# First kernels on VectorE with the lengths' tables behind them, later chunks' exponentials on GpSimd, and products of ones ahead of the first strip

## The chip, the cores and the metric

One core of a Trainium2 chip runs the whole program. The metric is the device time in microseconds (us), as the median of several runs. TensorE (PE) multiplies matrices, VectorE (DVE), ScalarE (ACT) and GpSimd (POOL) work on tiles of up to 128 partitions, and SyncE's queue (SP) issues most transfers.

## The reference

For 128 sequences (B) of 32 heads (H) and 512 positions (L) the reference does three things.

- It makes one convolution kernel of 512 taps for each head from a diagonal state space model: `K[h, l] = 2 Re sum_n Ct[h, n] exp(dtA[h, n] * l)` over 64 complex states n, with `dtA = (-exp(log_A_real) + i A_imag) * dt` and `Ct = C (exp(dtA) - 1) / A`.
- It convolves each row `x[b, h, :]` causally with `K[h]`, adds `D[h] * x`, and sets positions at and beyond the sequence's length to zero.
- It passes the 4096 rows of 512 values through a mixture of experts: sigmoid gates with a bias, the best 4 of 16 experts with normalised weights, a gated network `silu(x Wg) * (x Wu) Wd` of inner width 256 for each, plus one shared expert. The result is added to x.

```python
dtA = A * dt[:, None]
Ct = Cc * (jnp.exp(dtA) - 1.0) / A
P = dtA[:, :, None] * jnp.arange(length)
K = 2.0 * jnp.einsum('hn,hnl->hl', Ct, jnp.exp(P)).real
...
y = irfft(rfft(u, n=2*L) * rfft(K, n=2*L))[..., :L] + u * D[:, None]
y = y * mask[:, None, :]
...
out = x + experts(y)
```

## The kernel before

**Kernels of the heads.** States lie on partitions: 128 partitions hold the 64 states of two heads, so 32 heads are 16 column pairs. `CHUNKS = ((0, 2), (2, 4), (6, 4), (10, 6))` cuts these pairs into four chunks of 2, 4, 4 and 6, that is heads 0 to 3, 4 to 11, 12 to 19 and 20 to 31. A tap l is split into 16a + b, so that 32 + 16 = 48 values (`lab`) per pair are enough: a chunk's tiles are 128 x 96, 192, 192 and 288, and chunk 0 has 16 more columns in front (`lead`), from which `Ct` is made.

`waves` makes a chunk's exponentials. The angle part (L306, then `reduce_angle`, L244 to L248, then L316) works on `wr` and `wk` on VectorE, and ScalarE takes sine and cosine (L317, L322). The size part starts with a product on GpSimd (L309, into `wv`), goes through `exp_parts` on VectorE (L254 to L263: clamp, two steps for the exponent, two for the remainder, one for the scale `ws`, seven for the series `wq`) and ends in L325 (`wm`). All these tiles have one buffer. `kernels` then multiplies size by cosine and sine into `f_r`, `f_i` (L373, L374) and `ge_r`, `ge_i` (L381, L382), multiplies by `Ct` (L385 to L390, half of it on GpSimd), and TensorE sums over the states into `pk` (L394). VectorE adds the skip term into `krow` (L402), and SP writes it to DRAM as `kd` (L409). `kernel_strip` (L419) reads `kd` back as 128 shifted copies, the Toeplitz strip of four heads: in four transfers for heads 0 to 3, in one of 1 MB after that, with two buffers.

**The lengths' tables.** L429 to L512 rank the sequences by length, and make `to_rank`, `to_row`, `within` and, from them, `by_rank`, `reach`, `k_u` and `unit_rows`. The convolution needs only `within` and `to_rank`; `to_row` goes into `route`, and the others are used after the last head.

**The convolution.** It runs over 8 blocks (`tb`) of 4 heads. For each head TensorE multiplies four pieces of the transposed x with the strip (`py`, L520), VectorE masks by length (`yb`, L527), TensorE transposes with `to_rank` (`pt`, L530), and ScalarE copies to `store` (L531). After a block come the gates on TensorE (`parts` L549, `pg` L560), and after every second block `route` on VectorE, which finds the best four experts. Chunks 1, 2 and 3 are made after heads 0, 2 and 5 in the order of the program. Strip `tb + 1` is loaded at the first head of block `tb`.

**Order.** Up to the last head the order of each engine's instructions is not written out: a scheduler places each one at build time from the order of the program and its own estimate of when operands are ready. Each engine then runs its list strictly in that order. After the convolution come the shared expert in eight units, the table of slots, and the experts' tiles, with orders written out by hand. The change does not touch them, but for where four of their tables are made.

Of the kernel before, what the change touches and what calls it, by code (L numbers as in the profile page):

```python
# [38 lines left out]
P = 128  # L39
# [15 lines left out]
ONE_HOTS = 8  # L55
AHEAD = 4
# [19 lines left out]
def ssm_moe_kernel(  # L76
# [76 lines left out]


# [95 lines left out]
    def exp_parts(v, q, k, s):  # L250

        nc.vector.tensor_scalar(v, v, -87.0, 88.0, ALU.max, ALU.min)  # L254
        nc.vector.tensor_scalar(k, v, 1.0 / math.log(2.0), ROUND, ALU.mult, ALU.add)  # L255
        nc.vector.tensor_scalar(k, k, ROUND, None, ALU.subtract)
        for part in (LN2_1, LN2_2):
            nc.vector.scalar_tensor_tensor(v, k, -part, v, ALU.mult, ALU.add)
        nc.vector.tensor_scalar(q, v, SERIES[0], None, ALU.mult)
        for c in SERIES[1:]:  # L260
            nc.vector.scalar_tensor_tensor(q, q, c, v, ALU.add, ALU.mult)  # L261

        nc.vector.tensor_scalar(s, k, 127.0, 2.0**23, ALU.add, ALU.mult)  # L263
# [13 lines left out]
    def wide(name, w, dtype=F32, most=WMAX):  # L277
        return ks1.tile([P, most], dtype, tag=name, name=f"{name}{w}")[:, :w]
# [16 lines left out]
    def waves(c0, n, lead):  # L295
# [3 lines left out]
        v, r, k, q = (wide(t, w) for t in ("wv", "wr", "wk", "wq"))  # L299
        s, mag = wide("ws", w, I32), wide("wm", w)  # L300

        def pairs(t):
            return t[:, lead:].rearrange("p (c x) -> p c x", x=NX)

        by_l = lab.unsqueeze(1).to_broadcast([P, n, NX])
        nc.vector.tensor_mul(  # L306
            pairs(r), by_l, dta_i[:, c0 : c0 + n].unsqueeze(2).to_broadcast([P, n, NX])
        )
        nc.gpsimd.tensor_mul(  # L309
            pairs(v), by_l, dta_r[:, c0 : c0 + n].unsqueeze(2).to_broadcast([P, n, NX])  # L310
        )
        if lead:
            nc.vector.tensor_copy(r[:, :lead], dta_i)
            nc.vector.tensor_copy(v[:, :lead], dta_r)
# [8 lines left out]
        exp_parts(v, q, wide("we", w), s)  # L323
        s = s.bitcast(F32)
        nc.vector.scalar_tensor_tensor(mag, q, 1.0, s, ALU.add, ALU.mult)  # L325
        return tuple(pairs(t) for t in (mag, k, r)), (mag, q, s, r, half)

    first, (mag, q, s, r, half) = waves(*CHUNKS[0], NC2)
# [38 lines left out]
    def kernels(c0, n, mag, cos, sin):  # L367

        cs = slice(c0, c0 + n)

        for j in range(2):
            rows = slice(j * N, (j + 1) * N)
            nc.vector.tensor_mul(f_r[rows, cs, j, :], cos[rows, :, LA:], mag[rows, :, LA:])  # L373
            nc.gpsimd.tensor_mul(f_i[rows, cs, j, :], sin[rows, :, LA:], mag[rows, :, LA:])  # L374
# [6 lines left out]
        nc.vector.tensor_mul(e_r, cos[:, :, :LA], mag[:, :, :LA])  # L381
        nc.gpsimd.tensor_mul(e_i, sin[:, :, :LA], mag[:, :, :LA])  # L382
# [3 lines left out]
        nc.gpsimd.tensor_mul(g_t, e_i, by_i)  # L386
        nc.vector.tensor_add(g_r, g_r, g_t)
        nc.vector.tensor_mul(g_i, e_r, by_i)
        nc.gpsimd.tensor_mul(e_i, e_i, by_r)
# [12 lines left out]
        nc.vector.tensor_add(  # L402
# [7 lines left out]
        for h in range(2 * c0, 2 * (c0 + n)):  # L410
            kd_of[h] = kd[h - 2 * c0 : h - 2 * c0 + 1, :]

# [12 lines left out]
    kernels(*CHUNKS[0], *first)  # L425
    kernel_strip(0)


    len_col = const.tile([P, 1], F32, tag="len_col", name="len_col")  # L429
    nc.vector.tensor_copy(len_col, len_col_i)  # L430
    key_row = const.tile([P, B], F32, tag="key_row", name="key_row")
    nc.vector.tensor_copy(key_row, len_row_i)
    key_col = const.tile([P, 1], F32, tag="key_col", name="key_col")
    for key, raw, own in ((key_row, key_row, cpos), (key_col, len_col, ppos)):
        nc.vector.tensor_scalar(key, raw, 0.0, float(L), ALU.max, ALU.min)
        if key is key_col:
            num_len = const.tile([P, 2], F16, tag="num_len", name="num_len")
            nc.vector.tensor_copy(num_len[:, 0:1], ppos)
# [16 lines left out]
    to_rank_h = const.tile([P, P], F16, tag="to_rank_h", name="to_rank_h")  # L455
    nc.vector.tensor_copy(to_rank_h, to_rank)

    by_rank_ps = ps_m.tile([P, 2], F32, tag="m", name="by_rank_ps")
    nc.tensor.matmul(by_rank_ps, lhsT=to_rank_h, rhs=num_len, start=True, stop=True)
    by_rank = const.tile([P, 2], F32, tag="by_rank", name="by_rank")  # L460
    nc.vector.tensor_copy(by_rank, by_rank_ps)


    reach = const.tile([P, KT], BF16, tag="reach", name="reach")
    nc.vector.memset(reach, 1.0)
    for n in range(1, KT):
        nc.vector.tensor_scalar(
            reach[:, n : n + 1], by_rank[:, 1:2], float(n * P), None, ALU.is_gt
        )

    unit = const.tile([P, NU], BF16, tag="unit", name="unit")
    nc.vector.tensor_scalar(unit, upos, 0.0, None, ALU.is_equal)
    reach_sum = const.tile([P, 1], F32, tag="reach_sum", name="reach_sum")
    nc.vector.tensor_reduce(reach_sum, reach, AX.X, ALU.add)
    reach_b = const.tile([P, 1], BF16, tag="reach_b", name="reach_b")
    nc.vector.tensor_copy(reach_b, reach_sum)
    k_u_ps = ps_m.tile([1, NU], F32, tag="m", name="k_u_ps")
    nc.tensor.matmul(k_u_ps, lhsT=reach_b, rhs=unit, start=True, stop=True)
    k_u = const.tile([1, NU], I32, tag="k_u", name="k_u")
    nc.vector.tensor_copy(k_u, k_u_ps)  # L480


    div = const.tile([P, 2], F32, tag="div", name="div")
# [367 lines left out]
    def dep(of, on, why):  # L851
        tc.add_manual_dep(of.ins, on.ins.name, SYNC, reason=why)
# [345 lines left out]
```

## Time and profile before

| | |
|---|---|
| median of 3 runs | 956.56 us (956.15 to 957.12) |
| the profiled execution | 961.51 us, its span 959.8 us |
| last `pt` of the convolution done | about 139.5 us |
| `krow` of chunk 0 done, first `py` | 22.39 us, 27.09 us |
| busy over the span | PE 93%, VectorE 45%, GpSimd 45%, ScalarE 18% |
| granted TensorE clock, mean | 0.985 |

A row of the timeline has the start in us, the duration in us, engine, line, operation, output and inputs, and in brackets the idle time before it with what ended it. The rows of windows give, for each stretch, its length and the busy time of PE, PE weight loads, VectorE, ScalarE and GpSimd with their numbers of instructions, then the granted clock, the share of the transfer engines that was busy, and GB/s. The shares over the whole span say little here, since the change lies in the first 100 us.

### The profile page before, as it was taken

Reading aid. Unit: us, or ns where it says so; the run is one execution under the profiler, and the core shown is the slowest. Engines: PE = TensorE matmul, PEld = TensorE weight load, DVE = VectorE, ACT = ScalarE, POOL = GpSimd, SP = SyncE. Lnnn points to the kernel's source line nnn. Section 1 sums busy time; section 2 is a strip of 40 time slices with the busy share of each in tenths; the row PEclk is TensorE's granted clock in tenths of the full one; section 3 lists DMA queues with packets and bytes.
Section 4 is the critical chain, followed back from the end, with each engine's and each line's share of the span. In section 5 each row is a group of like instructions: output and inputs, shape, how many; then the busy total and the mean of one; then the engine's idle time right before and its main releaser. Section 6 shows DMA issues by size and latency. Waiting matters only on the chain.

```text
span 959.8 us, 14544 instructions
## 1 busy us (share of the span) xinstructions
PE 890.6 (93%) x2960; PEld 443.3 (46%) x2960; DVE 427.6 (45%) x1438; ACT 171.3 (18%) x343; POOL 432.0 (45%) x400
## 2 busy tenths in 40 slices
PE   0799994989998999999999999999999999999995
PEld 0455652344444444444444444444444544444442
DVE  7955555868762233443334233423433323334332
ACT  1122221000001012221222122212222112222211
POOL 4210002033456545664556455655555445556644
PEclk9999997989999999999999999999999999999998
DMA  4467732164456676687667766766666646677755
GB/s 161 126 228 265 233 125 68 66 223 151 165 193 196 251 166 111 127 138 164 113 119 140 166 109 120 137 108 106 125 121 114 112 90 113 112 119 138 131 110 104
DMA packets 54032, 135.94 MB, mean 142 GB/s; under 512 B 12784, under 2 KB 12944, under 8 KB 51344
## 3 DMA queue, kind: packets, MB, share of 16 engines
q0 software_dynamic: 35616, 89.77, 47.5%
q1 hardware_dynamic: 14064, 36.15, 11.4%
q10 hardware_dynamic: 4224, 8.39, 2.3%
q8 instruction: 71, 1.16, 0.5%
q14 instruction: 57, 0.47, 0.1%
HBM read 288.08 MB, written 52.25 MB: 355 GB/s over the span
## 4 chain that ended last, share of the span: by engine, by line
PE 78%; DVE 15%; issue 3%; another core or an unknown queue 1%; DMA 1%; POOL 1%; ACT 0%; SPq 0%; DVEq 0%; POOLq 0%; ACTq 0%
PE g L1044 33%; PE o L1070 24%; PE m L1012 4%; PE o L930 3%; PE u L1062 3%; PE py L520 3%; PE u L904 2%; DVE cols L794 2%; PE g L904 2%; DVE rows L793 1%; DVE yb L527 1%; PE pt L530 1%; DVE wq L261 1%; PE parts L549 1%
## 5 line engine op out<-in xcount | busy, mean ns | idle before, releaser
L1044 PE MATMUL g<-store,yt 128*128 x742 | 343.1, 596 | 4.1 <-ACT yt L1018 2.7
L1080 POOL DMA_INDIRECT out<-xg,put x134 | 212.1, 1583 | 236.5 <-DVE junk L1019 203.2
L1070 PE MATMUL o<-store,zT 128*128 x536 | 252.2, 593 | 1.3 <-DVE zT L1065 1.3
L1056 DVE SCALAR_TENSOR_TENSOR zt<-g,wt,sgt 128x256 f32<-128x256 f32 x135 | 65.3, 483 | 287.0 <-ACT sgt L1055 272.6
L1044 PEld LDWEIGHTS g<-store,yt 128*128 128x128 f32 x742 | 130.3, 190 | 121.0 <-issue 116.8
L1070 PEld LDWEIGHTS o<-store,zT 128*128 128x128 f32 x536 | 101.3, 190 | 130.5 <-issue 124.3
L869 POOL DMA_INDIRECT yg<-y_rows,get x140 | 138.8, 991 | 42.8 <-issue 30.2
L1079 DVE COPY xg<-o 128x512 f32<-128x512 f32 x134 | 92.7, 692 | 110.3 <-PE o L1070 109.4
L1018 ACT COPY yt<-m 128x512 f32<-128x512 f32 x136 | 79.6, 586 | 238.1 <-PE m L1012 225.9
L1055 ACT ACTIVATE sgt<-g 128x256 f32<-128x256 f32 x135 | 51.9, 384 | 268.6 <-PE g L1044 227.8
L1012 PEld LDWEIGHTS m<-ident,yg 128*128 128x128 f32 x373 | 48.5, 141 | 73.2 <-issue 73.0
L520 PE MATMUL py<-strip,xt 128*128 128x512 f32 (+3 forms) x256 | 77.7, 443 | 5.0 <-DMA strip<-kd 5.0
L918 POOL DMA_INDIRECT xg<-in_x,unit_rows x32 | 31.1, 970 | 108.9 <-DVE sig_k L255 99.5
L939 POOL DMA_INDIRECT out<-xg,unit_rows x32 | 31.5, 984 | 98.6 <-DVE xg L937 90.4
L930 PE MATMUL o<-store,z 128*128 128x512 f32 x128 | 60.5, 622 | 6.1 <-DVE xg L937 6.1
L1012 PE MATMUL m<-ident,yg 128*128 128x128 f32 x373 | 63.3, 273 | 1.1 <-issue 1.1
L1065 DVE COPY zT<-u 128x256 f32<-128x256 f32 x134 | 56.3, 420 | 0.1
L520 PEld LDWEIGHTS py<-strip,xt 128*128 128x128 f32 x256 | 41.9, 194 | 21.8 <-issue 9.3
L1062 PE MATMUL u<-ident,zt 128*128 128x128 f32 x268 | 51.2, 273 | 0.0
L904 PE MATMUL g<-store 128*128 128x512 f32 x92 | 44.5, 621 | 0.7 <-ACT store L531 0.7
L904 PE MATMUL u<-store 128*128 128x512 f32 x92 | 42.9, 601 | 0.8 <-issue 0.8
L930 PEld LDWEIGHTS o<-store,z 128*128 128x128 f32 x128 | 24.8, 199 | 38.0 <-issue 28.0
(272 smaller groups left out, 519.7 us busy)
## 6 DMA issues: line engine op xcount, KB each, us to landing
store<-in_w_all SPq DMA_DIRECT2D x143, 1536.0 KB
xt<-in_x_t SPq DMA_DIRECT2D x8, 1024.0 KB
y_rows<-yb ACTq DMA_DIRECT2D x8, 1024.0 KB
strip<-kd SPq DMA_DIRECT2D x7, 1024.0 KB
yg<-y_rows,get POOLq DMA_INDIRECT x140
out<-xg,put POOLq DMA_INDIRECT x134
strip<-kd SPq DMA_DIRECT2D x4, 256.0 KB
xg<-in_x,unit_rows POOLq DMA_INDIRECT x32
```

The costliest lines, as they stand in the source:

```text
L520: nc.tensor.matmul(py[:, : L - jt * P], lhsT=xt[:, jt, q, :], rhs=strip[tb][:, q, jt * P :], start=(jt == 0), stop=(jt == KT - 1),)
L869: nc.gpsimd.indirect_dma_start(out=at(yg, t), out_offset=None, in_=y_rows[:, :], in_offset=bass.IndirectOffsetOnAxis(ap=made["get"][:, t : ...
L904: nc.tensor.matmul(ps[it], lhsT=w_sh[:, c0 : c0 + P], rhs=yT[:, u, kt, :, :].rearrange("p h b -> p (h b)"), start=(kt == KT - n), stop=(kt ...
L930: nc.tensor.matmul(po, lhsT=at(zu, u)[:, it, q * P : (q + 1) * P], rhs=w_sh[:, c0 : c0 + L], start=(it == 0), stop=(it == IT - 1),)
L1012: nc.tensor.transpose(pt[:, q, :], at(yg, t)[:, q * P : (q + 1) * P], ident)
L1018: nc.scalar.copy(at(yt, t), pt)
L1044: mm = nc.tensor.matmul(pgu, lhsT=at(yt, t)[:, q, :], rhs=ring_flat[:, bass.ds(w0s[t] + q * 2 * I, 2 * I)], start=(q == KT - n), stop=(q = ...
L1056: nc.vector.scalar_tensor_tensor(at(zs, t), pgu[:, I:], at(wts, t), sg, ALU.mult, ALU.mult)
L1062: nc.tensor.transpose(at(p_z, t)[:, it, :], at(zs, t)[:, it * P : (it + 1) * P], ident)
L1070: mm = nc.tensor.matmul(po, lhsT=at(zts, t)[:, it, :], rhs=ring_flat[:, bass.ds(w0s[t] + WD + it * L, L)], start=(it == 0), stop=(it == IT ...
L1079: nc.vector.tensor_copy(ob, po)
L1080: add = nc.gpsimd.indirect_dma_start(out=out, out_offset=bass.IndirectOffsetOnAxis(ap=put[:, t : t + 1], axis=0), in_=ob, in_offset=None, ...
```

## The change

- Chunk 0 is made without GpSimd: the first product of the size part, `f_i`, `ge_i` and the two products with `Ct` go to VectorE.
- The size part of chunks 1 to 3 (`sizes`) goes to GpSimd as a whole. [...]24 instructions a chunk. `sizes` of chunk 1 has no wait of its own; that of chunk 2 and 3 waits for GpSimd's last product of the chunk before (`pool_last`).
- The angle part (`turns`) of chunks 1 to 3, and the lengths' tables that the convolution needs, wait for `krow` of chunk 0 (`behind`). The other tables (`ranks`) move to the start of block 2.
- VectorE's first products of chunks 1 to 3 in `kernels` wait for a masked head (`masked`). Chunks 2 and 3 are made after heads 7 and 15 in place of heads 2 and 5.
- Seven of the wide tiles have two buffers.
- After `krow` of chunk 0 TensorE runs 16 products of a tile of ones, 128 x 512, whose result nobody reads (`keep_warm`).

```diff
+WARM = 16
...
-    def exp_parts(v, q, k, s):
+    def exp_parts(v, q, k, s, on=None):
+        on = on or nc.vector
+        def times_plus(dst, a, c, b):
+            if on is nc.vector:
+                on.scalar_tensor_tensor(dst, a, c, b, ALU.mult, ALU.add)
+            else:
+                on.tensor_scalar(q, a, c, None, ALU.mult)
+                on.tensor_add(dst, q, b)
+        def plus_times(dst, a, c, b):
+            if on is nc.vector:
+                on.scalar_tensor_tensor(dst, a, c, b, ALU.add, ALU.mult)
+            else:
+                on.tensor_scalar(dst, a, c, None, ALU.add)
+                on.tensor_mul(dst, dst, b)
...
+        bufs = 2 if name in ("wv", "wr", "wk", "wq", "we", "ws", "wm") else 1
...
+    def sizes(c0, n, lead, on, behind=None):
+        first = by_steps(v, dta_r, c0, n, lead, on)
+        if behind is not None:
+            dep(first, behind, "one chunk behind the other")
+        plus_times = exp_parts(v, q, k, s, on)
+        plus_times(mag, q, 1.0, s)
...
+    def turns(c0, n, lead):
+        first = by_steps(r, dta_i, c0, n, lead, nc.vector)
+        if c0:
+            behind(first)
...
+    def next_sizes(c):
+        return sizes(*CHUNKS[c], 0, nc.gpsimd, behind=pool_last.get("e_i"))[0]
...
-    def kernels(c0, n, mag, cos, sin):
+    def kernels(c0, n, mag, cos, sin, behind=None):
+        other = nc.gpsimd if c0 else nc.vector
-            nc.vector.tensor_mul(f_r[rows, cs, j, :], cos[rows, :, LA:], mag[rows, :, LA:])
-            nc.gpsimd.tensor_mul(f_i[rows, cs, j, :], sin[rows, :, LA:], mag[rows, :, LA:])
+            first = nc.vector.tensor_mul(f_r[rows, cs, j, :], cos[rows, :, LA:], mag[rows, :, LA:])
+            if behind is not None:
+                dep(first, behind, "later in VectorE's order")
+            other.tensor_mul(f_i[rows, cs, j, :], sin[rows, :, LA:], mag[rows, :, LA:])
...
-        nc.gpsimd.tensor_mul(e_i, e_i, by_r)
+        pool_last["e_i"] = other.tensor_mul(e_i, e_i, by_r)
...
+    def keep_warm(behind_):
+        warm = ps_u.tile([P, KT, P], F32, tag="u", name="warm")
+        for n in range(WARM):
+            mm = nc.tensor.matmul(
+                warm,
+                lhsT=ones,
+                rhs=ones.unsqueeze(1).to_broadcast([P, KT, P]),
+                start=True,
+                stop=True,
+            )
+            dep(mm, behind_, "behind the first kernels")
...
-    kernels(*CHUNKS[0], *first)
+    chunk0 = kernels(*CHUNKS[0], *first)
+    pool_last.clear()
+    mag = next_sizes(1)
     kernel_strip(0)
+    keep_warm(chunk0)
+    def behind(op):
+        dep(op, chunk0, "later in VectorE's order")
...
-    nc.vector.tensor_copy(len_col, len_col_i)
+    behind(nc.vector.tensor_copy(len_col, len_col_i))
...
-    chunk_at = {0: CHUNKS[1], 2: CHUNKS[2], HB + 1: CHUNKS[3]}
+    chunk_at = {0: 1, 2 * HB - 1: 2, 4 * HB - 1: 3}
     for tb in range(NB):
+        if tb == 2:
+            by_rank, reach, k_u, unit_rows = ranks()
...
-            convolve(tb, q, xb, yb)
+            masked = convolve(tb, q, xb, yb)
             if tb * HB + q in chunk_at:
-                c0, n = chunk_at[tb * HB + q]
-                kernels(c0, n, *waves(c0, n, 0)[0])
+                c = chunk_at[tb * HB + q]
+                angles = turns(*CHUNKS[c], 0)[:2]
+                kernels(*CHUNKS[c], *waves(0, mag, *angles), behind=masked)
+                if c + 1 < len(CHUNKS):
+                    mag = next_sizes(c + 1)
```

## The prediction

> **What bounds the kernel now.** I read the page first (TensorE is busy for 93% of the span), then the stretches before TensorE fills, the waits of TensorE there, and the timeline row by row. Times are us from the span's start.
>
> The stretches up to the fifth head (`py` of head 4 starts at about 43.9: the x10 group of 42.58, less its last four products):
>
> ```profile
> 8.93:16.35 7.42, 0.79 (x5) 0.42 (x5) 7.41 (x56) 0.79 (x3) 1.43 (x5) 1.00 0.98 411
> 16.35:20.19 3.84, 0.07 (x1) 0.00 (x0) 3.79 (x30) 0.00 (x0) 1.20 (x4) 1.00 0.31 128
> 20.19:22.39 2.20, 0.85 (x8) 0.58 (x8) 1.83 (x11) 0.00 (x0) 0.88 (x2) 1.00 0.00 0
> 22.39:27.09 4.70, 0.00 (x0) 0.00 (x1) 4.07 (x14) 0.71 (x2) 0.66 (x2) 1.00 0.42 123
> 27.09:44.20 17.11, 14.07 (x77) 8.63 (x78) 16.34 (x56) 2.72 (x6) 5.31 (x12) 1.00 0.30 92
> ```
>
> The third column is VectorE: it is full up to `krow` of chunk 0 (22.39), and the work there is more than chunk 0 needs. Then TensorE waits for the first strip, and after that for masks:
>
> ```profile
> PE py L520 <- DMA strip<-kd: 5.0, 1, 5.0
> PE pt L530 <- DVE yb L527: 3.7, 3, 1.9
> ```
>
> From about 54 to 139 TensorE has no gaps, and the whole remainder hangs on it. So the change can win only what it takes from the first 54 us, and that passes to the end one for one. Three more sets of rows carry the sums. A chain of dependent instructions, the first head and a later pair of half heads:
>
> ```profile
> 24.03 2.32 DVE L261 SCALAR_TENSOR_TENSOR wq<-wq,wv 128x192 f32<-128x192 f32 x6
> 27.09 3.95 PE L520 MATMUL py<-strip,xt 128*128 128x512 f32 x8 [4.95 <-DMA strip<-kd]
> 59.84 2.32 PE L520 MATMUL py<-strip,xt 128*128 128x384 f32 x8
> ```
>
> Six dependent steps take 0.39 each, 0.05 over the 0.34 of one. The first head takes 3.95 for what takes 2.32 later, though the granted clock reads 1.00. VectorE and GpSimd meeting:
>
> ```profile
> 28.43 0.60 POOL L386 TENSOR_TENSOR gg_t<-ge_i,ct_i 128x128 f32<-128x128 f32 x1
> 28.69 0.48 DVE L385 TENSOR_TENSOR gg_r<-ge_r,ct_r 128x128 f32<-128x128 f32 x1
> 29.09 0.28 DVE L388 TENSOR_TENSOR gg_i<-ge_r,ct_i 128x128 f32<-128x128 f32 x1
> 29.10 0.53 POOL L389 TENSOR_TENSOR ge_i<-ge_i,ct_r 128x128 f32<-128x128 f32 x1
> 29.30 0.48 DVE L387 TENSOR_TENSOR gg_r<-gg_r,gg_t 128x128 f32<-128x128 f32 x1
> 29.70 0.28 DVE L390 TENSOR_TENSOR gg_i<-gg_i,ge_i 128x128 f32<-128x128 f32 x1
> ```
>
> The same VectorE operation is 0.28 alone and 0.48 beside GpSimd, and it ends 0.14 after GpSimd's does (29.03, 29.17). GpSimd in turn ends 0.26 after VectorE lets go (29.37, 29.63). They take turns, whole instructions at a time. And the way from `krow` to a strip:
>
> ```profile
> 34.79 0.33 SPq L409 DMA_DIRECT2D kd<-krow  x1
> 36.32 0.38 SPq L419 DMA_DIRECT2D strip<-kd  x1
> 40.00:41.00 1.00, 1.00 0.85 330
> 41.00:42.00 1.00, 1.00 0.04 16
> ```
>
> 1.5 for `kd`, then 4.6 for a strip of 1 MB (traffic ends at about 40.9).
>
> **The change part by part.**
>
> Chunk 0 alone on VectorE. In 8.93 to 16.35 its angle part has 9 instructions and its size part 16 at a width of 112; the rest is tables. The size chain alone is 9 two-tile steps at 0.32 (0.27 + 0.05) and 5 one-tile steps at 0.26, 4.2; the angles fill its pauses at some 0.07 each: 4.8, against 7.42. From 16.35 to 20.19 chunk 0 needs 21 products 16 wide, which start 0.09 apart where they are dense, and six of `f` and `e` at 0.12 to 0.15 (two of them brought over from GpSimd as `f_i`, one as `ge_i`): 2.9, against 3.84, in which chunk 1 had its share. 20.19 to 22.39 stays: two products more on VectorE, two waits for GpSimd (0.2 each) less. Gain 2.6 + 0.9 = 3.5: `krow` at 18.9, if nothing else happens.
>
> Sizes of chunk 1 on GpSimd, 24 instructions. Their first operand is there at 8.7 and the second buffers take away their old wait for `wq`, so they run just while VectorE makes chunk 0. What one holds the port for is 0.39 with two operands (0.26 x 192/128, ten of them). No row shows GpSimd's one-operand arithmetic; the nearest is its selection over 128 x 128, 283 ns, which less a start of 0.13 is 0.23 for 192 wide (fourteen); a fill (0.51 for 512) would give 0.17, the two-operand rate 0.39. The Trainium skill (SBUF — State Buffer, "SBUF: two separate sides") says of the pair's shared port that whichever of the two starts first keeps it for the whole instruction, and that the other blocks fully. It speaks against this change. Taken to the letter, all 24 holds fall on VectorE: 10 x 0.39 + 14 x 0.23 = 7.1, and `krow` comes at 26.0. The rows make it less: VectorE's own start of about 0.1 goes on under the wait, and where its instructions are dense GpSimd gets no turn (at 20.34 its 64-wide product took 0.55, and 0.35 at 17.36). At a GpSimd pitch of 0.5 plus a wait of 0.12, 16 of 24 fall before `krow`, at 0.28 less 0.1 each: 2.9. I go with the rows: `krow` at 21.8, 0.6 earlier than now, with 18.9 and 26.0 as ends (28.3 if one operand costs as much as two).
>
> Products of ones. The table's fp16 products, 143 wide, start 0.062 apart, so 512 wide is 0.22 at speed (an estimate) and 0.44 at the half speed that the first head shows (3.95 for 2.32, most of it in the first four products). The first head was slow for about 2.5. With eight of the 16 slow it is 8 x 0.44 + 8 x 0.22 = 5.3, against 4.7 from `krow` to the strip: they hold the first head back by 0.6 and spare it 1.6. Bounds 3.5 and 7.0. Queued behind them on TensorE are the two products of the rank, so VectorE waits for `rank` until about 27.2; `to_rank` is needed only at the first `pt` near 30.
>
> Tables and angles behind `krow`: 14 small instructions at about 0.2 and nine 192-wide ones at 0.3, some 5.5, in the 7.5 until the first mask. Covered; without the cover up to 1 on the mask. The later tables (`ranks`, some 25 at 0.1 to 0.2) move to block 2, where VectorE has lost three size parts (4.4, 4.4 and 5.5) and is idle more than half of the time (4.41 and 4.18 busy of 10 in 50 to 70). Nothing. The wait of one VectorE instruction on another costs what a dependence costs, 0.05.
>
> Chunk 1 behind mask 0. The first head runs 27.1 to 29.4 (`krow` 21.8 + 5.3), mask 0 ends at 30.1 (now 34.57). Then come seven products (27.42 to 29.98 now: 2.6; plus about 0.8, since sizes of chunk 2 run on GpSimd beside them), `pk` with its wait for a piece of a head 1.4, `krow` 0.5, `kd` 1.5, strip 4.6: 41.5. TensorE's own work, four heads, three `pt` and `pk`, would reach head 4 at 27.1 + 11.2 = 38.3. So head 4 waits 3.2 for its strip, and starts at 41.5 in place of 43.9: 2.4 earlier. That is the new last wait: the saved mask waits (3.7) and the warm clock come to no more than this.
>
> Here a second rule speaks: TensorE: Matmul & The Clock Gate ("Why this matters for your kernels") wants no pause over some 3 us, or the clock falls to half again. In the trace a pause of 1.9 before 34.63 left the next products at full speed; none of 3 with a warm clock before it is there. By the rows the pause costs its length only, by the rule 1.6 more. I take the rows.
>
> Chunks 2 and 3. From the end of a mask to the `py` five heads on there is 12.0 (mask 7 ends 59.2, head 12 starts at about 71.2). Needed: products 2.6 to 3.4, `pk` 1.5, `krow` 0.6, `kd` and strip 6.1: 10.8 to 11.6. Covered by about 1; in the sum 0.3 for a miss, up to 2 at each. SP's queue keeps its order of needs: the small `kd` writes move past one load of x (0.34 of issue) and strip 2; strip 3 now waits for `kd`, where it waited for a buffer (58.97). ScalarE's sines (0.5 and 0.4) and the `o` banks of `pk` are free there. Sizes of chunk 3 are done before `route` fills VectorE from 67; if not, each of the rest holds `route` by up to 0.6.
>
> Sum: 43.9 to 41.5 is -2.4. The last wait for a mask (0.62 at 52.7) goes and one `pk` of 0.6 comes after head 4 in place of before it: 0. The miss adds 0.3: -2.1. The profiled execution is 961.51 with a span of 959.8 (1.7 around it); it becomes 959.4. It lies 5 above the median of 956.56; the difference carries over to the median: 954.5.
>
> **The rivals.**
>
> - GpSimd gets out of the way. For it: dense VectorE code starves it. `krow` at 18.9, and head 4 is 2.9 + 2.4 earlier: 951.2. Against: VectorE's chain is one of dependent steps, with a pause after each.
> - GpSimd holds the port (slower). The place is chunk 0's chain on VectorE, the price 7.1 to 9.4 on `krow`: it comes at 26.0 to 28.3, and all after it moves by 4.2 to 6.5 from my forecast: 958.7 to 961. It decides from `krow` later than about 26. For it: the collision rows, and VectorE blocked from 5.15 to 6.77 by GpSimd's fills (a 32-wide step took 1.62). Against: there GpSimd's instructions were independent of each other, here each waits for the last.
> - Strips 3 and 5 come late: each chain over 12.0 costs its excess. At 2 each, with the rest as forecast: 958.
> - The change doesn't do what it says: the scheduler may put `krow` or chunk 1's products late in an engine's list, by its own estimate of GpSimd's speed. The strip of block 1 then comes where it came before relative to the first (head 4 at 16.8 after it): with `krow` 0.6 earlier, 956.
>
> **How the numbers follow.** Forecast 0.38 (953 to 956, 954.5), out of the way 0.15 (951), holds the port 0.27 (958.7 to 961), late strips or an unhelpful order 0.20 (956 to 958.5). 0.2%, 1.9 us, is about what a measurement of this kernel can tell from no change: faster means below 954.65, slower above 958.47. Faster takes somewhat over half of the forecast, 0.22, all of the second, 0.15, and 0.06 of the last for a half miss: 0.43. Slower takes the third, and 0.05 of the fourth: 0.32. Same 0.25. The forecast's own range is 953 to 956; over all cases 949.8 to 960.8.
>
> **What would show it.** Right: `krow` of chunk 0 ends at 20.5 to 23, with VectorE's one- and two-tile steps at 0.4 to 0.6 beside GpSimd; the first `py` group takes about 2.3; the one long wait of TensorE after it is for a strip, 2 to 4, before head 4. Wrong: `krow` at 19 with short VectorE rows, or after 26; no wait for a strip at head 4; waits of TensorE for strips at heads 12 and 20, or for masks between 60 and 80. It is wrong as a whole if the time after head 4 moves by other than head 4 does.

## The result: slower, with a later end of the convolution

The changed kernel takes 963.86 us (962.75 to 964.63, 4 runs) against 956.5 before (4 runs): ratio 1.0075, interval 1.0058 to 1.0093. I had predicted 954.5. Its profiled execution took 964.63 with a span of 962.8. The lines of the masked heads, before and after (last start in us behind "first and"):

```profile
L527 DVE TENSOR_TENSOR yb<-py,within x32: 672/690/692, 33.9 to 138.0; 128x512 f32<-128x512 f32 x32
```

```profile
L602 DVE TENSOR_TENSOR yb<-py,within x32: 627/690/692, 33.4 to 145.7; 128x512 f32<-128x512 f32 x32
```

The last head comes 7.7 later, the median 7.4: the loss arises ahead of the end of the convolution. The same holds for nearly every kernel below: the profiled execution's time less the start of its last mask is 817 to 820. Two cases stand apart: 823.5 in the profile of before, which is the 5 us by which it lies above its median (in g, the kernel before with one transfer split, the last mask is at 138.0 too, and the time 955.85), and 822.5 in both kernels of the last group of runs, where the kernel before took 961.4. So the start of the last mask is the measure in what follows, and a median is compared only with that of the kernel before in the same group. Each profile is one execution and need not lie at the median of its kernel: it is 0.8 above it in the changed kernel, 2.1 in a and 1.5 in b, and 2.2 below it in k and 1.3 in q. A difference of under some 2 us between two last masks is therefore not shown by the profiles alone.

The stretches that answer to those shown of before (first and second: the work up to `krow` of chunk 0, then up to the first `py`, then to 44.20):

```profile
8.82:16.57 7.75, 0.00 (x0) 0.00 (x0) 7.61 (x35) 0.79 (x3) 6.71 (x13) 1.00 1.00 422
16.57:22.99 6.42, 0.79 (x8) 0.58 (x8) 5.58 (x33) 0.00 (x0) 5.66 (x9) 1.00 0.11 42
22.99:28.07 5.08, 5.02 (x18) 2.00 (x19) 5.04 (x21) 0.00 (x0) 3.80 (x6) 1.00 0.48 138
28.07:44.20 16.13, 11.79 (x64) 7.14 (x63) 12.32 (x38) 3.96 (x9) 12.31 (x21) 1.00 0.28 88
```

VectorE has fewer instructions ahead of `krow` (68 in 14.2 us; before 97 in 13.5) and is still full, because GpSimd, the last busy column, is busy beside it. TensorE's waits from 24 to 165:

```profile
PE pt L605 <- DVE yb L602: 6.9, 5, 2.8
PE py L595 <- DMA strip<-kd: 1.7, 1, 1.7
...
PE pk L444 <- DVE gg_i L440: 0.5, 1, 0.5
PE pt L605 <- ACT wk L354: 0.5, 1, 0.5
PE pk L444 <- DVE gg_r L437: 0.4, 2, 0.2
```

Before, the same window had 4.5 for masks, 3.7 of it before 54 us, and 5.0 for the first strip, but nothing at all from 57 to 117. Now TensorE waits for masks mainly in two places, 2.8 at head 0 and 2.3 at heads 10 and 11, and for the strip of block 5.

**Where the time went.** The starts of eight masks (timeline, `yb` of heads 0, 4, ...), of before, after and the kernels of the experiments:

| kernel | 0 | 4 | 7 | 8 | 11 | 15 | 22 | 31 |
|---|---|---|---|---|---|---|---|---|
| before | 33.9 | 47.2 | 58.5 | 61.3 | 71.7 | 85.0 | 108.1 | 138.0 |
| after | 33.4 | 47.3 | 57.5 | 62.1 | 76.6 | 89.7 | 116.6 | 145.7 |
| a_dve_late | 26.8 | 47.0 | 56.0 | 59.6 | 70.5 | 84.7 | 111.6 | 140.8 |
| b_dve_early | 27.2 | 48.3 | 59.4 | 62.2 | 72.6 | 85.4 | 109.3 | 139.2 |
| d_two_op | 33.2 | 47.0 | 57.2 | 62.4 | 73.8 | 86.9 | 113.5 | 142.7 |
| i_size1_dve | 27.1 | 47.7 | 56.6 | 61.6 | 75.7 | 88.8 | 115.9 | 145.1 |
| n_size3_dve_7 | 33.4 | 47.7 | 57.9 | 61.5 | 74.3 | 87.6 | 114.4 | 143.6 |
| m_chunk3_at_13 | 33.4 | 47.4 | 57.5 | 62.2 | 76.7 | 89.2 | 114.8 | 144.0 |
| p_angles3_late | 31.7 | 45.1 | 55.2 | 59.8 | 74.4 | 88.1 | 116.6 | 145.7 |
| q_gpsimd_best | 32.0 | 45.2 | 56.3 | 59.1 | 71.0 | 86.9 | 109.9 | 139.8 |
| e_no_ones | 32.3 | 46.2 | 56.4 | 61.1 | 75.0 | 88.7 | 115.5 | 144.6 |
| f_split | 27.7 | 43.7 | 54.8 | 58.2 | 68.7 | 82.2 | 105.2 | 135.2 |
| o_split_4_12 | 27.1 | 40.9 | 51.4 | 54.2 | 64.6 | 80.5 | 103.5 | 133.4 |

After against before, stretch by stretch: up to head 7 it is 1.1 ahead; 7 to 8 costs 1.8, 8 to 11 costs 4.2, 11 to 15 gives 0.3, 15 to 22 costs 3.8, the rest gives 0.8. The lead of 1.1 is borrowed: at head 7 the kernel before had done all sums `pk`, the changed one still has those of chunks 2 and 3 ahead of it, 0.9 and 1.1 of TensorE's time (its busy time in the windows of these 16 and 24 products). With this work counted where it was before, the losses are 0.9 up to head 7 (2.0 less 1.1), 0.9 around chunk 2's `pk` (TensorE waits 0.7 of it for `gg_r` and `gg_i`), 4.2 over heads 8 to 11, and 2.7 over heads 15 to 22, of which the strip of block 5 has 1.7; the other 1.0 is not resolved.

**Heads 8 to 11.** `route` of the first two blocks starts on VectorE at 66.4, and GpSimd is in the sizes of chunk 3 from 52.8 to 75.2. Two steps of `route` before, the second row with six steps of the series, and then VectorE's timeline of after:

```profile
68.10 0.29 DVE L258 SCALAR_TENSOR_TENSOR neg<-sig_k,neg 128x128 f32<-128x128 f32 x1
69.51 1.91 DVE L261 SCALAR_TENSOR_TENSOR sig_q<-sig_q,neg 128x128 f32<-128x128 f32 x6
```

```profile
68.60 0.92 DVE L263 SCALAR_TENSOR_TENSOR neg<-sig_k,neg 128x128 f32<-128x128 f32 x1
...
70.55 1.42 DVE L271 SCALAR_TENSOR_TENSOR sig_q<-sig_q,neg 128x128 f32<-128x128 f32 x2
71.89 0.68 DVE L602 TENSOR_TENSOR yb<-py,within 128x512 f32<-128x512 f32 x1
72.49 2.02 DVE L271 SCALAR_TENSOR_TENSOR sig_q<-sig_q,neg 128x128 f32<-128x128 f32 x4
74.54 0.77 DVE L293 SCALAR_TENSOR_TENSOR neg<-sig_q,sig_s 128x128 f32<-128x128 f32 x1
```

The steps take up to three times as long (0.92 for 0.29), the six of the series 3.44 for 1.91, and masks stand between them in VectorE's list. TensorE waits, and then its clock falls (TensorE's timeline, and the windows, whose third number from the end is the granted clock):

```profile
72.71 0.63 PE L605 MATMUL pt<-to_rank,yb 128*128 128x128 f32 x4 [1.95 <-DVE yb L602]
73.18 3.82 PE L595 MATMUL py<-strip,xt 128*128 128x256 f32 x8
```

```profile
72.00:74.00 2.00, 1.29 (x9) 1.26 (x10) 1.93 (x4) 0.58 (x1) 1.83 (x3) 0.96 0.01 4
74.00:76.00 2.00, 2.00 (x4) 0.82 (x3) 1.86 (x5) 0.00 (x0) 1.78 (x4) 0.50 0.42 82
76.00:78.00 2.00, 1.61 (x7) 0.65 (x6) 1.97 (x10) 0.00 (x0) 1.67 (x4) 0.68 1.00 422
```

The head that takes 2.33 at speed took 3.82: 1.5 more behind a wait of 1.95.

**Block 5's strip.** The way from `krow` to the strip, from the timeline of after:

```profile
89.72 0.35 SPq L152 DMA_DIRECT2D xt<-in_x_t  x1
90.44 0.37 ACTq L922 DMA_DIRECT2D y_rows<-yb  x1
94.31 0.33 SPq L459 DMA_DIRECT2D kd<-krow  x1
100.40 0.36 SPq L470 DMA_DIRECT2D strip<-kd  x1
```

The waits of SP's own queue from 56 to 102 say what its strips waited for:

```profile
SPq L470 <- DMA kd<-krow: 10.3, 2, 5.7
```

Before, the strip of block 1 was issued 1.5 after its `kd`. Here it is 6.1 (5.0 at head 7), all of it waiting for that write, and the two transfers of 1 MB that head 15 starts, the next x and the store of y, are issued ahead of it.

### The profile page after: what moved, and what is told of

Same layout as the page of the kernel before. It is cut to its first block, busy times and chain, and to the rows that moved or that the text cites. A ratio compares the mean times of both kernels' runs of the same rounds, so it can differ in the third digit from the quotient of the medians.

```text
span 962.8 us, 14594 instructions
## 1 busy us (share of the span) xinstructions
PE 894.5 (93%) x2976; PEld 444.7 (46%) x2976; DVE 427.3 (44%) x1402; ACT 170.8 (18%) x343; POOL 478.1 (50%) x463
## 3 DMA queue, kind: packets, MB, share of 16 engines
q0 software_dynamic: 35616, 89.77, 47.2%
q8 instruction: 72, 1.18, 0.5%
## 4 chain that ended last, share of the span: by engine, by line
PE 81%; DVE 13%; issue 2%; DMA 1%; SPq 1%; POOL 0%; ACT 0%; DVEq 0%; POOLq 0%; ACTq 0%
PE g L1122 33%; PE o L1148 24%; PE o L1008 5%; PE m L1090 4%; PE u L982 4%; PE py L595 3%; PE u L1140 3%; PE g L982 3%; DVE cols L870 2%; DVE yb L602 1%; DVE rows L869 1%; PE pt L605 1%; PE parts L625 1%; DVE sig_q L271 1%; DVE z L1044 1%
## 5 line engine op out<-in xcount | busy, mean ns | idle before, releaser
L1157 DVE COPY xg<-o 128x512 f32<-128x512 f32 x134 | 92.6, 691 | 109.3 <-PE o L1148 109.3
L1090 PEld LDWEIGHTS m<-ident,yg 128*128 128x128 f32 x373 | 48.6, 141 | 72.8 <-issue 72.6
L595 PEld LDWEIGHTS py<-strip,xt 128*128 128x128 f32 x256 | 41.5, 193 | 17.3 <-issue 11.3
```

The costliest lines, as they stand in the source:

```text
L595: nc.tensor.matmul(py[:, : L - jt * P], lhsT=xt[:, jt, q, :], rhs=strip[tb][:, q, jt * P :], start=(jt == 0), stop=(jt == KT - 1),)
L1090: nc.tensor.transpose(pt[:, q, :], at(yg, t)[:, q * P : (q + 1) * P], ident)
L1157: nc.vector.tensor_copy(ob, po)
```

## The experiments

All against the kernel before in the same group of runs, with the 95% interval of the ratio.

| run | median us | before | ratio |
|---|---|---|---|
| after | 963.86 | 956.5 | 1.0075 (1.0058 to 1.0093) |
| a_dve_late | 958.56 | 956.88 | 1.0018 (1.0009 to 1.0026) |
| b_dve_early | 957.09 | 956.88 | 1.0003 (0.9994 to 1.0012) |
| c_free0 | 970.11 | 956.88 | 1.0144 (1.0127 to 1.0161) |
| e_no_ones | 963.62 | 956.88 | 1.0072 (1.0055 to 1.0089) |
| d_two_op | 961.74 | 957.14 | 1.0045 (1.0029 to 1.0062) |
| f_split | 952.91 | 957.14 | 0.9952 (0.9935 to 0.9968) |
| g_before_split | 957.16 | 957.14 | 1.0003 (0.9994 to 1.0012) |
| h_split_no_ones | 953.73 | 957.14 | 0.996 (0.9946 to 0.9974) |
| i_size1_dve | 963.42 | 956.7 | 1.0079 (1.0062 to 1.0096) |
| j_size3_dve | 964.68 | 956.7 | 1.0063 (1.0037 to 1.0089) |
| k_heads_6_14 | 963.12 | 956.7 | 1.0068 (1.0051 to 1.0085) |
| l_late_split | 954.36 | 956.7 | 0.9972 (0.9962 to 0.9981) |
| m_chunk3_at_13 | 963.79 | 957.08 | 1.0071 (1.0054 to 1.0088) |
| n_size3_dve_7 | 962.4 | 957.08 | 1.0053 (1.0036 to 1.0069) |
| o_split_4_12 | 952.21 | 957.08 | 0.995 (0.9933 to 0.9967) |
| p_angles3_late | 967.96 | 961.39 | 1.0064 (1.0047 to 1.0081) |
| q_gpsimd_best | 963.69 | 961.39 | 1.0023 (1.0012 to 1.0033) |

**Sizes off GpSimd (a), and the chunks back at their old heads (b).**

```diff
-        return sizes(*CHUNKS[c], 0, nc.gpsimd, behind=pool_last.get("e_i"))[0]
+        return sizes(*CHUNKS[c], 0, nc.vector, behind=chunk0)[0]
...
-    chunk_at = {0: 1, 2 * HB - 1: 2, 4 * HB - 1: 3}     # b only
+    chunk_at = {0: 1, 2: 2, HB + 1: 3}
```

> The changed kernel with the sizes of chunks 1 to 3 on VectorE, their first product behind krow of chunk 0; all else stays (ones, tables behind, chunks 2 and 3 after heads 7 and 15). If GpSimd's sizes are the cause (port), krow of chunk 0 comes at 18.5 to 19.5 in place of 22.99, the mask waits around 72 and the half clock at 74 to 76 go, and the time falls by 5 to 8, to 956 to 959. If the late chunks are the cause, krow comes early too, but strips 3 and 5 stay late (issued 5 to 6 behind their kd) and the time stays above 960.

> As the kernel with sizes on VectorE, and with chunks 2 and 3 after heads 2 and 5 again. Port theory: within 2 of the kernel with sizes on VectorE and late chunks (late chunks cost 0 to 2), 953 to 957. Late-chunk theory: this one alone comes down, to about 955, and the other stays above 960.

`krow` of chunk 0 ends at 18.88 in both, where the changed kernel has 22.99. Of these 4.1 us 0.4 are an earlier start: `dn`, from which chunk 0 is made, ends at 8.58 in a and at 9.01 in the changed kernel. In c, below, it ends at 9.02, and none of GpSimd's `sizes` stands ahead of `krow`. The rows of `krow` in the changed kernel and in c:

```profile
22.78 0.21 DVE L452 TENSOR_TENSOR krow<-pk,dsk 32x64 f32<-32x64 f32 x1 [0.69 <-PE pk L444]
```

```profile
19.10 0.21 DVE L452 TENSOR_TENSOR krow<-pk,dsk 32x64 f32<-32x64 f32 x1 [0.69 <-PE pk L444]
```

So GpSimd's company costs chunk 0 3.7 us. Mask 0 comes 6.6 earlier in a and 6.2 in b. Yet of the 7.4 a still has 1.7 and b 0.2, and neither is faster than before. The table of masks shows where the lead goes: at head 4 nothing is left of it. In a TensorE waits there for the strip of block 1:

```profile
40.75 3.33 PE L595 MATMUL py<-strip,xt 128*128 128x512 f32 x4 [2.54 <-DMA strip<-kd]
```

That strip is issued at 34.17, the next x at 36.74, and the granted clock is 0.50 from 40 to 46. In b the strip is issued at 34.63, but TensorE stands at chunk 2's sums first (1.66 for `gg_r`, up to 40.75), so that the two can't be told apart there. The windows of b show what a thin stretch brings on:

```profile
38.00:40.00 2.00, 0.63 (x4) 0.42 (x4) 1.97 (x7) 0.88 (x3) 1.40 (x4) 1.00 1.17 294
40.00:42.00 2.00, 0.98 (x15) 0.85 (x16) 1.41 (x6) 0.00 (x0) 0.87 (x2) 0.60 0.92 246
42.00:44.00 2.00, 2.00 (x8) 0.99 (x6) 1.91 (x8) 0.00 (x0) 0.00 (x0) 0.50 0.98 392
44.00:46.00 2.00, 2.00 (x5) 1.01 (x3) 1.32 (x4) 0.00 (x0) 0.00 (x0) 0.50 1.05 380
```

TensorE is busy 1.61 of 4 us, and then runs at half clock for nearly 7 (windows of half a us read 0.50 from 40.5 to 47).

**Chunk 0 free of GpSimd, by a wait (c).** The sizes of chunk 1 stay on GpSimd, but start behind `krow` of chunk 0:

```diff
+    pool_last["e_i"] = chunk0
     mag = next_sizes(1)
```

> The changed kernel with GpSimd's sizes of chunk 1 behind krow of chunk 0, so that the port is free for chunk 0. Port theory: krow of chunk 0 at 18.5 to 19.5 and the first py near 24; but GpSimd's 17.6 then end at about 37, so head 4 waits for its strip until about 46, and sizes of chunk 3 meet the first route for longer: 963 to 967. If the port doesn't matter for chunk 0: krow stays at 22 to 23 and the time rises by 4 or more.

`krow` ends at 19.31, and the time is the worst of all. VectorE's timeline names the reason:

```profile
38.47 0.46 DVE L321 TENSOR_TENSOR wr<-lab,dta_i 128x288 f32<-128x288 f32 x1 [9.50 <-POOL ge_i L432]
38.84 0.68 DVE L603 TENSOR_TENSOR yb<-py,within 128x512 f32<-128x512 f32 x1
```

The angle product of chunk 3 stands ahead of mask 0 in VectorE's list and needs the buffer of `wr` that chunk 1 holds until GpSimd has read it for `ge_i`. The changed kernel has the same row with a smaller number:

```profile
31.57 0.46 DVE L321 TENSOR_TENSOR wr<-lab,dta_i 128x288 f32<-128x288 f32 x1 [1.05 <-POOL ge_i L432]
...
33.39 0.68 DVE L602 TENSOR_TENSOR yb<-py,within 128x512 f32<-128x512 f32 x1
```

**That wait taken away (p).**

```diff
-        if c0:
+        if c0 == 10:
+            dep(first, masks[4], "behind mask 4")
+        elif c0:
             behind(first)
...
+            masks.append(masked)
```

> The changed kernel with one wait changed: the angle part of chunk 3 waits for the mask of head 4 instead of the first kernels' sum. In the changed kernel its first product stands ahead of mask 0 in VectorE's list and waits for GpSimd's ge_i of chunk 1, which still holds the buffer; TensorE waits 2.8 us for that mask. If this is why mask 0 is late, mask 0 starts at 30.5 to 32.4 instead of 33.4, everything up to head 7 comes 1 to 2.5 us earlier, and the time is 961 to 963. If mask 0 is late because of VectorE's other work, nothing moves: 963 to 964.5.

Mask 0 comes 1.7 earlier and head 7 2.3 earlier: the cause of the late mask was right. Ahead of mask 0 VectorE's list still has later tables (`ranks`), which the program has in block 2. The lead is 1.6 at head 15 and gone at head 22, where TensorE waits 1.9 for the strip of block 5 and the granted clock is 0.89 over 104 to 120. The end does not move.

**The ones (e, h).** e is the changed kernel and h the later kernel f, both without `keep_warm(chunk0)`.

> The changed kernel without the 16 products of ones. If they cost (they hold the two products of the rank and the first head back by 0.6 to 1): 1 faster. If they pay by the clock: the first head takes 3.9 in place of 2.3 and the time is 0 to 1.5 slower; since mask 0 comes late for another reason (VectorE stands behind the angles of chunk 3), the most likely is no change within 1: 963 to 965.

> The kernel with the four transfers and all sizes on VectorE, without the products of ones. If the ones keep the clock up for the first head, the first head runs at half clock and it is 0.5 to 1.5 slower than with them; if they only hold TensorE, it is up to 0.6 faster; if the masks on VectorE set the pace of the first heads anyway, within 0.3 of it.

The ones do what they are for. In h the first twelve products (a head and a half) take 6.88, with the ones 3.88 in f (TensorE's timelines of h and f):

```profile
23.88 6.88 PE L594 MATMUL py<-strip,xt 128*128 128x512 f32 x12 [0.93 <-DMA strip<-kd]
```

```profile
25.13 3.88 PE L595 MATMUL py<-strip,xt 128*128 128x512 f32 x12
```

But the mask of head 3 starts at 37.9 in h and 38.1 in f, and the intervals of both pairs overlap: masks and strips set the pace there, not TensorE.

In the changed kernel the ones also have a price. The two products of the rank stand behind them on TensorE, VectorE gets the rank 3.6 later than in e, and the later tables ahead of mask 0 wait for it (VectorE's timelines of after and of e):

```profile
29.86 0.15 DVE L520 COPY rank<-rank_ps 128x1 f32<-128x1 f32 x1
```

```profile
26.28 0.14 DVE L519 COPY rank<-rank_ps 128x1 f32<-128x1 f32 x1
```

Mask 0 starts at 32.3 in e and at 33.4 in the changed kernel, and the same 1.1 stands between their last masks. The medians, 963.62 and 963.86, do not show it.

**GpSimd's steps by form (d).**

```diff
-                on.tensor_scalar(q, a, c, None, ALU.mult)
+                on.tensor_scalar(q, a, c, 0.0, ALU.mult, ALU.add)
...
-                on.tensor_scalar(dst, a, c, None, ALU.add)
+                on.tensor_scalar(dst, a, c, 1.0, ALU.add, ALU.mult)
```

and likewise the rounding step and the first of the series.

> The changed kernel with GpSimd's one-operation steps written as two operations (a product plus 0.0, a sum times 1.0); the clamp and the two-operand steps as they are. If the form sets their length, as the 0.69 us of a one-operation step against 0.35 us of a two-operation one of the same 128x192 suggests, a chunk's sizes take about 11 to 13 us instead of 17.6 and chunk 3's about 14 to 16 instead of 22.4: they end before route starts at 66, route's steps on VectorE lose their holds, and the time falls by 3 to 5, to 959 to 961. The first kernels' sum ends 1 to 2 us earlier too, if shorter steps hold VectorE less. If the length comes from the step's data and not its form, nothing changes: 963 to 965.

The groups by form, of after and of d (mean ns is the last number before the idle time):

```profile
L273 POOL TENSOR_SCALAR wq<-wq 128x192 f32<-128x192 f32 x12 | 8.6, 716 | 1.0
L273 POOL TENSOR_SCALAR wq<-wq 128x288 f32<-128x288 f32 x6 | 5.6, 938 | 0.5
```

```profile
L273 POOL TENSOR_SCALAR wq<-wq 128x192 f32<-128x192 f32 x12 | 4.5, 373 | 1.0
L273 POOL TENSOR_SCALAR wq<-wq 128x288 f32<-128x288 f32 x6 | 2.8, 466 | 0.5
```

The form sets the length: with two operations written out the same step takes half the time on the mean. Chunk 3's sizes end at 66.1 instead of 75.2, `route` runs nearly free, heads 8 to 11 take 11.4 instead of 14.5, and the last mask comes 3.0 earlier. One point fell: `krow` of chunk 0 does not come earlier but at 24.4. All 24 steps now fall ahead of it, and they still hold VectorE: `dn` ends at 8.60 as in a, and `krow` comes 5.5 later than there, 0.23 for a step; in the changed kernel it is 3.7 for 18 steps, 0.20. These are means over steps of all forms.

**Which chunk's sizes cost (i, j, n).** i has those of chunk 1 on VectorE, j and n those of chunk 3: j behind chunk 0's sum, n behind chunk 2's.

```diff
+        if c == 1:                                        # i; c == 3 in j and n
+            return sizes(*CHUNKS[c], 0, nc.vector, behind=chunk0)[0]   # n: behind=last_krow
         return sizes(*CHUNKS[c], 0, nc.gpsimd, behind=pool_last.get("e_i"))[0]
```

> The changed kernel with the sizes of chunk 1 on VectorE behind the first kernels; those of chunks 2 and 3 stay on GpSimd. All three on VectorE gave 5.3 back. If it is GpSimd's hold on the first kernels that costs, this run alone gives that back: krow ends near 18.9 and the time is 958 to 959.5. If the first kernels' lead is lost at head 4 anyway, because its strip isn't there, and the cost lies in chunk 3's sizes beside route, then krow ends near 18.9 too but the time stays at 962 to 964.

> The changed kernel with the sizes of chunk 3 on VectorE; those of chunks 1 and 2 stay on GpSimd. The same two readings the other way round: if chunk 3's sizes beside route are the cost, TensorE's waits of 1.95 and 0.39 us for masks at 72.7 and 77.4 and the half clock behind them go, and the time is 959.5 to 961; VectorE takes on some 6 us of its own for it, part of which may show as waits for masks. If the hold on the first kernels is the cost, it stays at 962.5 to 964.

> The changed kernel with the sizes of chunk 3 on VectorE, this time behind chunk 2's sum at head 7: the other kernel with them on VectorE let them run from 36 us, ahead of the masks of heads 1 to 4, and so swapped one wait for another. If chunk 3's sizes on GpSimd beside route are a main part of the loss, route's steps are at their own length again, no half clock follows, and the time is 959.5 to 961.5 even with 6 us more on VectorE between heads 7 and 12. If they are not, 963 to 965.

i starts the first head like a, and its last mask is 0.6 before the changed kernel's, its ratio 1.0079 against 1.0075: the hold on the first kernels, of which the prediction made most, costs nothing at the end. In i TensorE waits 2.42 for the strip of block 1 before head 4, and the next four products take 3.33, as in a. n brings heads 8 to 11 down by 1.7 and the last mask by 2.1. There the steps of `route` are at their own length again (0.22 to 0.29 for those ahead of the series), but share VectorE with the sizes: TensorE still waits 1.80 and 0.27 for masks, and what is gone is the half clock behind them; its ratio, 1.0053 (1.0036 to 1.0069), overlaps the changed kernel's, so the row and not the median carries this. j tells nothing: VectorE ran the sizes from 36 us on, ahead of early masks, the granted clock was 0.66 over 36 to 40 and 0.63 over 48 to 52, and its five times reach from 959.9 to 965.4.

**The late writes of the kernels (k, m).** k puts chunks 2 and 3 behind heads 6 and 14, m chunk 3 behind head 13.

> The changed kernel with the kernels of chunks 2 and 3 behind heads 6 and 14 instead of 7 and 15. If the writes of the kernels to memory take 5 and 6 us instead of 1.5 because an x load and a store of y, 1 MB each, are issued right ahead of them behind heads 7 and 15, then one head earlier they land in 1.5 to 2.5, the wait of 1.7 for the strip of block 5 goes, and the time falls by 1.5 to 2.5, to 961.3 to 962.3. If it is something else, the writes take as long and it stays within 0.7 of the changed kernel's 963.9.

> The changed kernel with the kernels of chunk 3 behind head 13 instead of 15. Behind head 14 their write to memory still stood behind an x load of 1 MB on SP's queue and took 8.7 us to the strip's issue, so head 14 did not tell. Behind head 13 it is issued ahead of that load. If the load ahead is the cause, write and strip's issue lie 1.5 to 2.5 apart, TensorE's wait of 1.7 for the strip of block 5 goes, and the time is 1.5 to 2 less, 961.9 to 962.4. If the write is slow for another reason, the gap stays at 5 or more and the time at 963 to 964.5.

In k the write still stands behind the x load, which is issued at 58.70 and 87.44, and takes 6.1 and 8.7; TensorE's wait for the strip of block 5 stays at 1.7. In m it does so too, contrary to what I expected (x load at 89.20, write at 91.36, strip at 98.52), but the strip is issued 1.9 earlier. No wait of TensorE for that strip is left, and the last mask comes 1.75 earlier. The median did not follow (963.79); a gain of that size lies within its interval. That a write issued ahead of the load is quick is seen in o below.

**The strip in four transfers (f, g, l, o).** All sizes on VectorE, and the strip of block 1 fetched head by head, as that of block 0 is:

```diff
-        each = 1 if tb == 0 else HB
+        each = 1 if tb <= 1 else HB
```

> The changed kernel with all sizes on VectorE and the later chunks at heads 1, 3 and 6 as in the kernel before, and with the strip of block 1 fetched as four transfers of one head each instead of one. Theory late strip: head 4 waits for that strip whatever the first kernels do, because its one transfer of 1 MB shares the queues with an x load and a store of y; with four, head 4 starts when the first quarter is there, about 37.5 instead of 42, the pause of 4 us and the half clock behind it go, and the time is 949 to 952. Rival: the transfers' total is the bound and not the first quarter, then heads 4 to 7 each wait a part, and it stays at 955 to 957.

> The kernel before with the strip of block 1 fetched as four transfers, a control. There head 4 has its strip in time, so both theories expect no change: 956 to 957. If it gains 2 or more, the split helps for a reason of its own and the gain of the run beside it does not speak for the late strip.

> Both cures at once without GpSimd: all sizes on VectorE, chunks 2 and 3 behind heads 6 and 14, and the strip of block 1 in four transfers. If the late strip of block 1 and the late writes are all that keeps the later chunks' place from being as good as the early one, it comes to within 0.7 of the early placement with four transfers, 952.5 to 953.5; if the later place has a price of its own (the products of a chunk's kernels on TensorE among the heads, steps beside route), 954 to 956.

> All sizes on VectorE, the strip of block 1 in four transfers, and chunks 2 and 3 behind heads 4 and 12, where their writes stand ahead of an x load. VectorE is full from 28 to 56 with them behind heads 2 and 5, and TensorE stands 0.7 to 1.0 of every 4 us in it. If VectorE's load there is what remains, this spreads it and gains 0.5 to 1.5 on the early placement, 951.5 to 952.5; if the steps only move to where route needs VectorE, 952.9 to 954.

f takes the chunks at the old heads (as b), l at heads 6 and 14, o at 4 and 12. g is the kernel before with the split alone. TensorE's timeline of f at head 4:

```profile
38.40 1.10 PE L595 MATMUL py<-strip,xt 128*128 128x512 f32 x2 [0.75 <-DMA strip<-kd]
```

A wait of 0.75 at 38.4 in place of the one that ended at 40.75 in a, a granted clock of 1.00 in all windows from 34 to 50, and half a per cent off b (0.9952 against 1.0003). In the kernel before the split changes nothing, since there the strip is in time. So the first kernels' lead is worth something only once that strip lets it pass. l comes out behind f (0.9972 against 0.9952, the intervals overlap): its writes again stand behind x loads, and its strips follow them by 6.1 and 8.8. In o the write goes first:

```profile
80.00 0.32 SPq L459 DMA_DIRECT2D kd<-krow  x1
80.47 0.37 SPq L152 DMA_DIRECT2D xt<-in_x_t  x1
81.68 0.36 SPq L470 DMA_DIRECT2D strip<-kd  x1
```

1.7 from write to strip. o is the fastest kernel here, 0.995 of the kernel before; f is within its interval.

**All cures with the sizes on GpSimd (q).** The changed kernel with d's steps, the chunks at heads 4 and 12, and p's wait.

> The changed kernel with all cures that leave the sizes on GpSimd: its steps as two operations, chunks 2 and 3 behind heads 4 and 12 so that the writes of the kernels stand ahead of an x load and GpSimd is done before route, and chunk 3's angles behind mask 4. If the losses found (route beside GpSimd 3 to 4, the late strip 1.7, mask 0 about 1) are the whole of it, it comes to 956 to 958.5, about the kernel before. If GpSimd's hold has a price that these do not cover, 959 to 962. To the 952 of the version without GpSimd it comes only if the hold is worth nothing.

The last mask comes at 139.8, 5.9 before the changed kernel's, and the ratio is 1.0023: the cures account for most of the loss. By the last masks 1.8 of it remains against before, and 6.4 against o, which has the sizes on VectorE and the split; by the ratios it is about 2.2 and 7.0. The kernel before takes 4.5 more in this group than in the others, so that the 963.69 stand for 959.2 there: the second of the two outcomes that I had named, with a price that the cures do not cover.

## Why the prediction was wrong, step by step

The step that cost most is the pace of GpSimd: a step of `sizes` every 0.62 us was forecast, and 0.74 and, for chunk 3, 0.93 were measured, so that the sizes of chunk 3 ran beside `route`, which the prediction had put at nothing and which cost 4.2 us. The cover of mask 0 and the allowance for the late writes of chunks 2 and 3 failed besides. One by one:

- **Chunk 0 alone on VectorE: right.** 18.9 forecast, 18.88 measured where GpSimd keeps away.
- **GpSimd's hold: right in kind, small in size.** Forecast 2.9 (16 steps of 0.18), measured 3.7 (18 of 0.20); `krow` ended at 22.99 against 21.8, 0.4 of it by the later start. The 16 was a slip: it counts steps up to 18.9, and up to 21.8 the forecast's own pitch gives 21. That the count came out near is luck, since the true pitch was longer. The Trainium skill's rule (SBUF — State Buffer, "SBUF: two separate sides") taken to the letter gave 26.0. The rows lay nearer; that the hold was larger than they made it is the side to which the rule points. But i shows that this step is worth nothing at the end. VectorE's 112-wide step, which takes 0.27 alone (at 12.18 in a), beside a product on GpSimd (timelines of after):

```profile
13.73 0.59 POOL L266 TENSOR_TENSOR wv<-wq,wv 128x192 f32<-128x192 f32 x1
13.80 0.64 DVE L271 SCALAR_TENSOR_TENSOR wq<-wq,wv 128x112 f32<-128x112 f32 x1
```

- **GpSimd's own speed: the step that failed first.** I took 0.23 for what a one-operand step holds and 0.5 plus 0.12 as the pitch. The pitch was 0.74 (24 steps in 17.75): eleven steps are of one operation and took 0.69 to 0.82, and d shows that it is this form that makes them long. At 288 wide the pitch was 0.93.
- **"Sizes of chunk 3 are done before `route` fills VectorE from 67": wrong**, by that pitch, and no sum of its own stood behind it. They ended at 75.2. I had named the price (up to 0.6 a step) but put it at nothing. It was 4.2 over heads 8 to 11, some 1.5 of it half clock; d and n give 3.1 and 1.7 of it back.
- **Ones: right in their own row.** 5.10 measured, 5.3 forecast; the first head fast. That the rank stands behind them was seen and put at nothing; in the changed kernel it moved mask 0 by 1.1 (e).
- **Mask 0: wrong.** "Covered" at 30.1, measured 34.07 (start 33.39). The cover was counted in VectorE's busy time; its list was not looked at. A product that waits for GpSimd (c, p) and later tables that wait for the rank (e) stood ahead of the mask.
- **Head 4 at 41.5, set by its strip: the mechanism right, and not reached.** The changed kernel was late for another reason (its head 4 starts at 44.8). In a and i, where it wasn't, the strip is the wall, as forecast.
- **The pause: I chose the rows, and the clock did fall.** The wait of 2.54 before head 4 in a was followed by a granted clock of 0.50 over 40 to 46, so such a pause costs more than its length: the next four products took 3.33, where the same four took 1.74 behind the strip of block 5 in the changed kernel. The rule that I had cited, of pauses over some 3 us, is not enough either: 0.50 also followed a wait of 1.95 at 72.7, and 1.61 busy in 4 us in b. No fall followed the wait of 2.8 at head 0 in the changed kernel, and one followed the wait of 2.35 at the same head in n (0.73 over 32 to 36). The Trainium skill (TensorE: Matmul & The Clock Gate, "Part 1: The HAM clock gate") has the clock set by activity over a window of about 3.4 us that runs freely. A window that runs freely would look like that; no run here shows the window itself.
- **Chunks 2 and 3: too small.** The 6.1 for `kd` and strip came from a row with an idle queue. Behind x and y they are 5.0 to 6.1 for `kd` alone. I had allowed 0.3, "up to 2 at each"; it was 2.7 over heads 15 to 22, with 1.7 of it for the strip of block 5, and 0.9 around chunk 2's sums.

Against the forecast of -2.1 the end moved by +7.7: heads 0 to 7 missed by about 3.3 (2.4 earlier forecast, 0.9 later measured), heads 8 to 11 by 4.2, strip and sums by 3.3 (3.6 less the 0.3 allowed), less 1.1 won elsewhere. No rival had this sum. The nearest, GpSimd holding the port at chunk 0, named the right engine and the wrong place. What is left open: the last 1.8 to 2.2 of q, 1.0 over heads 15 to 22, and what exactly makes the clock fall.

## What to carry to other kernels

An engine that takes over work needs its own row for each form of each instruction before its end is put on a time axis; a neighbour that is slower than thought does its harm where it now overlaps, not where it was meant to. Ask of each saved microsecond which transfer it runs into next: here the first kernels' lead was worth nothing until one strip was fetched head by head, and then half a per cent. A lead is only a lead with the work counted that was put off.

## What the runs showed of the hardware that I had not expected

- GpSimd's multiply or add of a tile with one constant takes 0.72 us at 128x192 and 0.94 at 128x288 on the mean of the series' steps (L273); the same written as two operations (plus c, times 1.0) takes 0.37 and 0.47 (d). A clamp by max and min, two operations as well, takes 0.9 and 1.18.
- Shorter steps did not hold VectorE less: chunk 0's chain lost 0.23 us for each of 24 steps in d and 0.20 for each of 18 in the changed kernel.
- A write of 16 or 24 KB issued behind a load and a store of 1 MB each lets its successor go after 5.0 and 6.1 us (after), and issued ahead of the load after 1.7 (o).
